# A scan and a mixture of experts on one core: decays, matrix copies, late transfers and the first expert products in another order

## The chip, the cores and the metric

The kernel runs on one core of a Trainium2 chip. The metric is the device time in microseconds of one execution, measured on that core. Three executions of the kernel before were timed; one more was recorded by the hardware profiler.

The core has five instruction streams: PE (TensorE: matrix products, transposes), DVE (VectorE), ACT (ScalarE), POOL (GpSimd) and SP (SyncE, which here only issues transfers). Each runs its own instructions strictly in order, and waits on semaphores for the others. Transfers run on 16 DMA engines. There are two sources of transfers: plain ones, issued by SP, and indirect ones (gathers and scatters of rows by a list of indices), issued by POOL.

## What is computed

`x` is 2 sequences of 4096 tokens with 512 channels, in fp32. A layer norm is followed by two branches: `s`, a long convolution of each channel with a kernel made of 16 decaying exponentials, plus a scaled residual; and `g`, the SiLU of a mixture of experts (8 experts of 512 x 512 with a bias, the two best per token, weighted by a softmax). The output is `x + s * g`.

```python
def _L0_attn_ref(x, delta, alpha, beta, gamma, omega):
    scale = math.sqrt(1.0 / n_state)
    residual = x * omega
    p = jax.nn.sigmoid(delta)
    a = jax.nn.sigmoid(alpha)
    q = 1.0 - p * a
    vander = t[None, None, :] * jnp.log(q)
    kernel = p * beta * jnp.exp(vander)
    k = jnp.einsum('dnl,dn->dl', kernel, gamma * scale)
...
    out = jnp.fft.irfft(x_f * k_f, n=n_fft)[..., :l]
    return jnp.swapaxes(out, -1, -2) + residual

def _L0_ffn_ref(x, We, be, Wg, bg):
    gate_logits = xf @ Wg.T + bg
    topk_vals, topk_idx = jax.lax.top_k(gate_logits, TOP_K)
    gate_w = jax.nn.softmax(topk_vals, axis=-1)
    all_out = jnp.einsum('nd,ehd->neh', xf, We) + be
    sel = jnp.take_along_axis(all_out, topk_idx[:, :, None], axis=1)
    out = jnp.sum(sel * gate_w[:, :, None], axis=1)
...
xn = _layernorm(x, axis=-1)
s = _L0_attn_ref(xn, ...)
g = _silu(_L0_ffn_ref(xn, ...))
x = x + s * g
```

## The kernel before

**Three stages.** The first (about 0 to 100 us) loads `x`, normalises it into the tile `big`, and computes the gate's logits. The second (about 100 to 274 us) is the convolution, while DVE sorts the tokens by expert beside it. The third goes through the experts in 71 tiles of 128 tokens for every token's best expert, and 71 more for the second best.

**The convolution's loop.** The 512 channels are 64 *groups* `g` of 8 channels; four groups make a *set* `u` (16 sets, `i` is the group's place in its set). Every chunk of 64 tokens is multiplied with a 64 x 64 Toeplitz matrix of its channel (`from_chunks`: 16 products, which the profile shows as 32), and what earlier chunks left comes in through 16 states a channel: `states` (products into `ph`) makes a chunk's contribution, DVE multiplies it into `came` and runs two scans over it with the *decays*, and `from_states` adds the scanned states to the outputs `pys` of the *next* set. Once a set, at `i == 1`: `from_states(u)`, `powers_of(u + 2)` on ACT, `states(u + 1)`, the scans for `u + 1`, and `decay_of(u + 2, n)` on ACT, which writes over the decays that scan `n` has just read. At `i == 3`, `turn_powers` transposes the powers on PE and ACT copies them (`w <- pw`). At the set's end `outputs_end` copies the four output banks out of PSUM, three on ACT and one on DVE; a later set's products need those banks.

**The matrices.** `load_toep(g)` loads a group's matrices from DRAM into one half of the partitions (128 KB, issued by SP five groups ahead; six buffers). `double_toep(g)` copies them into the other half, on ACT or on POOL, as `TO_ACT` says by the group's place in its set. It is called two groups ahead, after the products of group `g - 2`.

**Transfers beside the loop.** The dictionary `between`, filled by `at(group, function, ...)`, says what is issued after which group. `store(qi, part)` writes a sixteenth of a quarter of the convolution's output to `s_dram` (256 KB, 64 x 8 rows of 512 bytes). `load_expert(e, half)` loads half of an expert's weights (512 KB) into the parts of `big` that the loop no longer needs. `load_bias(e)` loads a bias, broadcast to all partitions (256 KB), into the first half of the region of `big` from which the third quarter's parts 0 to 7 are stored; the second half, parts 8 to 15, later holds the first tiles' rows and normalised rows. So these loads wait for those stores. All of them stand in SP's one queue with the matrices' loads, in the order in which they are issued. `fetch(i)` is POOL's gather of tile `i`'s rows. Tiles 0 and 1 (`EARLY`) are fetched, normalised and transposed while the loop is still running.

**The experts.** A pass `i` of the loop at the end issues, in this order: `fetch(i + 7)`, statistics of rows (`mean_of`, DVE and ACT), `end_first(i - 2)` (DVE adds the bias to a finished product, POOL scatters the result to `yx_dram`), `normalise` (DVE) of tiles up to a few ahead, `turn` (PE transposes a normalised tile two or three ahead, ACT copies it) and `expert(i)` (PE, four products of 128 x 128 x 512). The normalising runs ahead as far as tile 3 in pass 0, 5 in pass 1, 6 in pass 2 and 8 in pass 3; from pass 4 on the turning runs three tiles ahead instead of two, so that pass 4 turns tiles 6 and 7 ahead of tile 4's product. The expert's number is read at run time, so a product can use any of the eight weights, and a bias addition any of the eight biases: both wait until all of them are there. Products go to five PSUM banks, which are the convolution's banks before.

All engines' instructions are issued through `InOrder`, which keeps the order of the program on each engine; so most lines of the profile bear the number of its one recording line, 59, and are told apart by their tiles.

Of the kernel before, what the change touches and what calls it, by code (L numbers as in the profile page):

```python
# [8 lines left out]
FP = mybir.dt.float32  # L9
# [7 lines left out]
P = 128  # L17
EPS = 1e-5
SX = 4
DOUBLED = 2  # L20
TO_ACT = (0, 2)
IL = 2
AHEAD = 7
READY = 5
# [38 lines left out]
def tile_ssm_then_moe(  # L63
# [179 lines left out]
    def turn(i, pt):  # L243
        xn = xn_b[i % len(xn_b)]
        for k in range(KD):
            io.tensor.transpose(pt[:, k, :], xn[:, k * P : (k + 1) * P], ident)
        io.scalar.copy(xnT_b[i % len(xnT_b)], pt.rearrange("p k t -> p (k t)"))
# [95 lines left out]
    with ExitStack() as ab:  # L343
# [63 lines left out]
        def decay_of(u, n):  # L407

            g = u * NS + 2 * n
            decay = work.tile([P, 2, NP * 2 * C], FP, tag="decay")  # L410
            for i in range(2):
                io.scalar.activation(
                    decay[:, i, :], carry.rearrange("p s c -> p (s c)"), AF.Copy,
                    scale=q_half[:, g + i : g + i + 1],
                )
            return decay


        def turn_powers(u, powers):

            pw = ps_w.tile([P, NS, P], FP, tag="hw", name="pw")
            for i in range(NS):
                io.tensor.transpose(pw[:, i, :], powers[:, i, 0:P], ident)
            w = work.tile([P, NS, P], FP, tag="w", bufs=1)
            io.scalar.copy(w, pw)
            return w
# [60 lines left out]
        def outputs_end(u, sq, pys):  # L487
            to = sq.rearrange("p c (s i r d) -> p s r i d c", i=NS, r=NR, d=NP)
            for r in range(NR):
                copy = io.vector.tensor_copy if r == 1 else io.scalar.copy  # L490
                copy(
                    to[:, u * NS % GQ // NS, r].rearrange("p i d c -> p c i d"),
                    pys[r].rearrange("p i d c -> p c i d"),
                )
# [440 lines left out]
        def load_bias(e):  # L935
            io.sync.dma_start(out=be_sb[:, e, :], in_=b_e[:, e, :].to_broadcast([P, D]))
# [6 lines left out]
        def sq_of(qi):  # L943
            return big[:, (4, 0, 4, 0)[qi], :].rearrange("p (c d) -> p c d", d=QD)
# [13 lines left out]
        def at(n, f, *args):  # L958
            between.setdefault(n, []).append((f, args))
# [19 lines left out]
        for part in range(NC):  # L979
            for qi in range(2):  # L980
                at(GQ * (qi + 1) + part, store, qi, part)
            at(GQ * 3 + part // 2, store, 2, part)
        for e in range(NE):
            for half in range(2):
                n = 2 * e + half
                at(GQ * 2 + 1 + 2 * n if n < NE else GQ * 3 + n, load_expert, e, half)
            at(GQ * 3 + NC // 2 + e // 2, load_bias, e)
        for i in range(EARLY):
            at(G - 6, fetch, i)
            at(G - 4 + i, mean_of, i)  # L990
# [5 lines left out]
        for u in range(NU):  # L996
            pys = banks() if u else pys0

            late = 0 if u else 1
            for i in range(2 * late, NS):  # L1000
                g = u * NS + i
                if g + TB - 1 < G:
                    toeps[g + TB - 1] = load_toep(g + TB - 1)
                if i == 1 + late:
                    from_states(u, pys, powers.pop(u))
                    if u + 2 < NU:
                        powers[u + 2] = powers_of(u + 2)
                    if u + 1 < NU:
                        states(u + 1, w.pop(u + 1))
                        for n in range(2):  # L1010
                            scan(n, decay.pop((u + 1, n)))
                            if u + 2 < NU:
                                decay[u + 2, n] = decay_of(u + 2, n)
                todo = between.pop(g, [])
                for f, args in todo:
                    if f in first_of_group:
                        f(*args)
                if i == 3 and u + 2 < NU:
                    w[u + 2] = turn_powers(u + 2, powers[u + 2])
                from_chunks(u, i, pys, toeps.pop(g))  # L1020
                if g + DOUBLED < G:
                    double_toep(g + DOUBLED)
                for f, args in todo:
                    if f not in first_of_group:
                        f(*args)
            outputs_end(u, sq_of(u * NS // GQ), pys)
        assert not between, between
        for part in range(NC):
            store(3, part)

    with ExitStack() as cc:
        mp = cc.enter_context(tc.tile_pool(name="more", bufs=1))
        ps_t = cc.enter_context(tc.tile_pool(name="ps_t2", bufs=2, space=PSUM))
        ps_e = cc.enter_context(tc.tile_pool(name="ps_e", bufs=5, space=PSUM))
        ps_tab = cc.enter_context(tc.tile_pool(name="ps_tab", bufs=1, space=PSUM))

        def more(n, width, name):
            return [mp.tile([P, width], FP, name=f"{name}{i}") for i in range(n)]

        xn_b += more(2, D, "xn")  # L1040
        xnT_b += more(3, D, "xnT")
        yx_b += more(4, 2 * D, "yx")
        sg_b += more(6, D + SX, "sg")
        x_b += more(FIRST - 5, D, "x")

        n = len(work_list)  # L1050
        for i in range(EARLY, AHEAD):
            fetch(i)
        ready, turned, ended, held = EARLY, EARLY, 0, {}

        def make_ready(upto, before_ends):

            nonlocal ready
            for i in range(ready, min(upto, n - 1) + 1):
                if before_ends:
                    if i < NT:  # L1060
                        mean_of(i)
                else:
                    normalise(i)
                    ready = i + 1

        def made_in_spare(b):

            low, high = (buf.bitcast(BF) for buf in (y_b[b % 2], g_b[b % 2]))
            return [
                low[:, 0 : BC * P].rearrange("p (c t) -> p c t", c=BC),  # L1070
                low[:, BC * P : BC * (P + NT)].rearrange("p (c t) -> p c t", c=BC),
                high[:, 0 : BC * 2 * NT].rearrange("p (c f t) -> p c f t", c=BC, f=2),
            ]

        late = list(range(NT, NT + AHEAD + 1))
        for before_ends in (True, False):
            make_ready(2, before_ends)
        for i in range(n + 1):
            if i + AHEAD < n:
                fetch(i + AHEAD)  # L1080
            to_be = i + 3 + min((i + 1) // 2, READY - 3)
            make_ready(to_be, True)
            ends = range(ended, i - (BEHIND if i < n - 2 else 1) + 1)
            ended = max(ended, ends.stop)
            for e in ends:
                if e < NT:
                    end_first(e, held.pop(e))
                elif e == ends[0]:
                    add_expert(e, held.pop(e))
            if ended >= NT:  # L1090
                for ii in late[: 3 if len(late) > AHEAD else 1]:
                    late.remove(ii)
                    fetch_first(ii)
                if i + AHEAD < n:
                    fetch_first(i + AHEAD)
            make_ready(to_be, False)
            if 0 <= i - TABLES - 2 < NM:
                put(ps_tab)
                if i - TABLES - 2 == NM - 1:
                    table_end(1, y_b[2][:, 0 : 2 * NT].rearrange("p (f j) -> p f j", f=2))  # L1100
            if 0 <= i - TABLES < NM:
                make(1, i - TABLES, made_in_spare)
            for ii in range(turned, min(i + 2 + (i >= 4), n - 1) + 1):
                turn(ii, ps_t.tile([P, KD, P], FP, name="pt"))
                turned = ii + 1
            if i < n:
                held[i] = ps_e.tile([P, D], FP, tag="pe", name="pe")
                expert(i, held[i])
            if ended == NT and ends:
                take_first(NT)  # L1110
                add_bias(NT)
                take_first(NT + 1)
            for e in ends:
                if e >= NT:
                    if e > ends[0]:
                        add_expert(e, held.pop(e))
                    if e + 1 < n:
                        add_bias(e + 1)
                    if e + 2 < n:
                        take_first(e + 2)  # L1120
                    put_out(e)
# [47 lines left out]
```

## Time and profile before

| | us |
|---|---|
| median of 3 executions | 874.09 (872.93 to 882.62) |
| the profiled execution | 874.42 |
| its span, first to last instruction | 872.7 |

```profile
PE 794.3 (91%) x7038; PEld 464.0 (53%) x7038; DVE 598.4 (69%) x1147; ACT 359.6 (41%) x699; POOL 507.4 (58%) x513
PE   3989888888974999999999999998998999999993
POOL 6777310333324357765455456767777777777752
PEclk9899999999997899999999999999999999999997
DMA  4656112889999974456555557668877777888851
```

The first line gives every engine's busy time, share of the span and number of instructions. Below it the span is cut into 40 equal slices of 21.8 us: a digit is the busy share of a slice in tenths, and for PEclk the TensorE clock that was granted. DMA is the mean busy share of the 16 DMA engines. The convolution is in the fifth to the thirteenth slice, the experts' first pass begins in the fourteenth, and the second pass follows it. The DMA engines are at nine tenths or more from the tenth slice to the fourteenth.

The issues, by kind, with the size of one and the median time from issue to landing:

```profile
s_dram<-big SPq DMA_DIRECT2D x64, 256.0 KB, 5.6
toep_b<-k_dram SPq DMA_DIRECT2D x64, 128.0 KB, 4.6
big<-in_w_e SPq DMA_DIRECT2D x16, 512.0 KB, 7.1
big<-in_b_e SPq DMA_DIRECT2D x8, 256.0 KB, 8.6
k_dram<-came_b SPq DMA_DIRECT2D x1, 256.0 KB, 2.3
```

### The profile page before, as it was taken

To read this page: it belongs to the slowest core of one execution; us is meant where nothing else is said; L and a number is where in the kernel's file an instruction comes from. 1 tells how busy PE (TensorE), PEld (TensorE's weight loads), DVE (VectorE), ACT (ScalarE), POOL (GpSimd) and SP (SyncE) were. 2 spreads that over 40 slices of the span, in tenths; PEclk is the share of its full clock that TensorE was granted. 3 is DMA by queue.
4 is the path that set the end of the run, shared out by engine and by line. 5 is a ranking of instruction groups with operands and counts; after the bars stand their busy time and mean duration, and the time that the engine had idled before them with its cause. 6 is when DMAs were issued, how large, how long until landed. Compare 5 with 4: busy or idle time off the path is not lost.

```text
span 872.7 us, 18657 instructions
## 1 busy us (share of the span) xinstructions
PE 794.3 (91%) x7038; PEld 464.0 (53%) x7038; DVE 598.4 (69%) x1147; ACT 359.6 (41%) x699; POOL 507.4 (58%) x513
## 2 busy tenths in 40 slices
PE   3989888888974999999999999998998999999993
PEld 3777777777763455554444445444443444444441
DVE  7878479766683667776566565355787777777786
ACT  6887666575652212222212212133443343433442
POOL 6777310333324357765455456767777777777752
PEclk9899999999997899999999999999999999999997
DMA  4656112889999974456555557668877777888851
GB/s 153 221 210 228 33 45 58 109 211 264 253 237 342 293 235 176 169 176 226 194 203 196 184 203 227 218 219 293 251 250 228 256 255 233 254 253 250 260 198 42
DMA packets 112823, 181.23 MB, mean 208 GB/s; under 512 B 18910, under 2 KB 68446, under 8 KB 112736
## 3 DMA queue, kind: packets, MB, share of 16 engines
q0 software_dynamic: 38128, 127.05, 44.1%
q1 hardware_dynamic: 74608, 52.99, 22.6%
q8 instruction: 58, 0.95, 0.4%
q14 instruction: 29, 0.24, 0.1%
HBM read 112.50 MB, written 73.01 MB: 213 GB/s over the span
## 4 chain that ended last, share of the span: by engine, by line
PE 36%; POOL 17%; issue 15%; DMA 14%; DVE 9%; ACT 8%; SPq 2%; POOLq 0%; DVEq 0%; ACTq 0%
PE pe L59 21%; POOL big L59 6%; PE py L59 5%; POOL out L59 5%; PE pt L59 4%; ACT big L59 4%; DVE came_b L59 4%; DMA yx<-yx_dram,x_idx 3%; DVE big L59 3%; DMA big<-yx_dram,x_idx 3%; POOL sg L59 3%; PE ph L59 2%; DMA toep_b<-k_dram 2%; SPq L59 2%; POOL yx L59 2%
## 5 line engine op out<-in xcount | busy, mean ns | idle before, releaser
L59 PE MATMUL pe<-big,xnT 128*128 x672 | 302.7, 593 | 0.4 <-issue 0.4
L59 PE MATMUL pe<-big 128*128 x464 | 212.0, 600 | 2.2 <-DMA s_dram<-big 2.2
L59 PEld LDWEIGHTS pe<-big,xnT 128*128 128x128 f32 x672 | 121.2, 190 | 122.1 <-issue 122.0
L59 PEld LDWEIGHTS pe<-big 128*128 128x128 f32 x464 | 85.1, 193 | 88.9 <-issue 85.8
L59 ACT ACTIVATE big<-big 128x512 f32<-128x512 f32 x103 | 66.5, 650 | 158.8 <-DVE big L59 154.3
L59 ACT COPY big<-pt 128x512 f32<-128x512 f32 x122 | 68.3, 594 | 90.8 <-PE pt L59 90.8
L59 ACT COPY xnT<-pt 128x512 f32<-128x512 f32 x84 | 48.4, 577 | 130.9 <-PE pt L59 130.4
L59 PE MATMUL py<-big,toep_b 64*64 64x64 f32 x2048 | 83.6, 231 | 20.3 <-ACT toep_b L59 8.3
L59 POOL DMA_INDIRECT out<-big,o_idx x71 | 78.5, 1105 | 39.2 <-DVE big L59 21.2
L59 PEld LDWEIGHTS pt<-ident,big 128*128 128x128 f32 x544 | 73.2, 195 | 49.8 <-issue 24.6
L59 PE MATMUL pt<-ident,big 128*128 128x128 f32 x544 | 86.9, 297 | 8.4 <-DVE big L59 5.8
L59 PEld LDWEIGHTS py<-big,toep_b 64*64 64x64 f32 x2048 | 72.9, 141 | 32.6 <-ACT toep_b L59 10.1
L59 POOL DMA_INDIRECT yx_dram<-big,o_idx x47 | 48.3, 1029 | 57.6 <-DVE big L59 51.2
L59 POOL COPY toep_b<-toep_b 64x512 f32<-64x512 f32 x32 | 23.2, 729 | 79.6 <-DMA toep_b<-k_dram 68.3
L59 POOL TENSOR_SCALAR big<-big,stats 128x512 f32<-128x512 f32 x44 | 55.7, 1343 | 23.5 <-ACT stats L59 9.8
L59 POOL DMA_INDIRECT big<-in_x,x_idx x52 | 51.0, 982 | 26.9 <-issue 13.8
L59 DVE TENSOR_TENSOR big<-pe,big 128x512 f32<-128x512 f32 x47 | 32.5, 691 | 42.4 <-PE pe L59 40.8
L59 PEld LDWEIGHTS pt<-ident,xn 128*128 128x128 f32 x280 | 33.7, 143 | 46.8 <-issue 30.9
L59 POOL DMA_INDIRECT sg<-s_dram,x_idx x42 | 47.2, 1125 | 12.8 <-issue 9.5
L59 PE MATMUL pt<-ident,xn 128*128 128x128 f32 x280 | 43.1, 278 | 11.9 <-DVE xn L59 10.9
L59 DVE TENSOR_TENSOR big<-big 128x512 f32<-128x512 f32 x73 | 50.3, 689 | 3.4 <-ACT big L59 1.9
L59 POOL DMA_INDIRECT big<-yx_dram,x_idx x44 | 43.4, 987 | 14.5 <-issue 13.1
(170 smaller groups left out, 1121.4 us busy)
## 6 DMA issues: line engine op xcount, KB each, us to landing
big<-in_x_rev SPq DMA_DIRECT2D x16, 1024.0 KB, 5.4
s_dram<-big SPq DMA_DIRECT2D x64, 256.0 KB, 5.6
toep_b<-k_dram SPq DMA_DIRECT2D x64, 128.0 KB, 4.6
big<-in_w_e SPq DMA_DIRECT2D x16, 512.0 KB, 7.1
big<-in_b_e SPq DMA_DIRECT2D x8, 256.0 KB, 8.6
out<-big,o_idx POOLq DMA_INDIRECT x71, 4.6
big<-in_x,x_idx POOLq DMA_INDIRECT x52, 3.5
yx_dram<-big,o_idx POOLq DMA_INDIRECT x47, 3.4
```

The costliest lines, as they stand in the source:

```text
L59: return lambda *args, **kwargs: self.order.follow(make(*args, **kwargs))
```

## The change

There are four edits. Their common effect on the engines' totals is nil: every instruction and every transfer stays, on another engine or in another place.

1. *Decays.* `decay_of(u + 2, n)` is issued in the set's fourth group, in front of `turn_powers`, and no longer right behind the scans in the second group.
2. *Copies of matrices.* ACT now copies the matrices of a set's second and third group (`TO_ACT` was the first and third), POOL those of the first and fourth. The copy for the next set's second group, which is called in the fourth group, is issued behind `outputs_end`.
3. *Late transfers.* In groups 48 to 63 the stores of the third quarter are issued one every second group, then one a group, and only parts 12 to 15 and 8 to 11; the experts' weights keep their step of one half every second group to the end of the loop (group 63). Parts 0 to 7 and, behind them, all eight biases are issued after the loop, in front of the fourth quarter's 16 stores.
4. *First expert products.* In passes 0 and 1, `expert(i)` is issued in front of the turning, so that tile 0's product stands before tile 2's turning on PE.

```diff
-TO_ACT = (0, 2)
+TO_ACT = (1, 2)
...
         for part in range(NC):
             for qi in range(2):
                 at(GQ * (qi + 1) + part, store, qi, part)
-            at(GQ * 3 + part // 2, store, 2, part)
+
+        for n, part in zip((0, 2, 4, 6, 7, 8, 9, 10), (12, 13, 14, 15, 8, 9, 10, 11)):
+            at(GQ * 3 + n, store, 2, part)
         for e in range(NE):
             for half in range(2):
                 n = 2 * e + half
-                at(GQ * 2 + 1 + 2 * n if n < NE else GQ * 3 + n, load_expert, e, half)
-            at(GQ * 3 + NC // 2 + e // 2, load_bias, e)
+                at(GQ * 2 + 1 + 2 * n, load_expert, e, half)
...
                             scan(n, decay.pop((u + 1, n)))
-                            if u + 2 < NU:
-                                decay[u + 2, n] = decay_of(u + 2, n)
...
                 if i == 3 and u + 2 < NU:
+                    for n in range(2):
+                        decay[u + 2, n] = decay_of(u + 2, n)
                     w[u + 2] = turn_powers(u + 2, powers[u + 2])
                 from_chunks(u, i, pys, toeps.pop(g))
-                if g + DOUBLED < G:
+                if g + DOUBLED < G and i < 3:
                     double_toep(g + DOUBLED)
...
             outputs_end(u, sq_of(u * NS // GQ), pys)
+            if g + DOUBLED < G:
+                double_toep(g + DOUBLED)
         assert not between, between
+        for part in range(NC // 2):
+            store(2, part)
+        for e in range(NE):
+            load_bias(e)
         for part in range(NC):
             store(3, part)
...
-            for ii in range(turned, min(i + 2 + (i >= 4), n - 1) + 1):
-                turn(ii, ps_t.tile([P, KD, P], FP, name="pt"))
-                turned = ii + 1
-            if i < n:
-                held[i] = ps_e.tile([P, D], FP, tag="pe", name="pe")
-                expert(i, held[i])
+
+            for what in ("turn", "expert") if i >= EARLY else ("expert", "turn"):
+                if what == "turn":
+                    for ii in range(turned, min(i + 2 + (i >= 4), n - 1) + 1):
+                        turn(ii, ps_t.tile([P, KD, P], FP, name="pt"))
+                        turned = ii + 1
+                elif i < n:
+                    held[i] = ps_e.tile([P, D], FP, tag="pe", name="pe")
+                    expert(i, held[i])
```

## Prediction

> **What bounds the kernel now.** I began with the table of forty slices on the page: PE is busy at 0.8 or more nearly everywhere, and its one hole is the two slices from 240 to 284 us (7 and 4 tenths), where the scan's loop hands over to the experts. So I asked for that hole's windows, then for the timelines of PE, SyncE (SP), GpSimd (POOL) and VectorE (DVE) in it.
>
> ```profile
> 240.00:250.00 10.00, 8.46 (x263) 7.02 (x262) 7.14 (x15) 6.31 (x15) 2.25 (x2) 1.00 1.05 244
> 260.00:270.00 10.00, 4.59 (x112) 4.08 (x114) 2.90 (x9) 2.07 (x4) 0.62 (x2) 0.76 1.05 287
> 270.00:280.00 10.00, 4.21 (x78) 3.72 (x75) 3.74 (x8) 2.99 (x7) 6.08 (x7) 0.84 1.05 382
> 280.00:290.00 10.00, 5.94 (x11) 2.95 (x12) 6.06 (x18) 1.76 (x5) 2.13 (x3) 0.54 1.04 329
> 290.00:300.00 10.00, 10.00 (x33) 4.97 (x32) 7.08 (x16) 2.52 (x7) 4.43 (x5) 1.00 1.01 272
> ```
>
> The columns after the stretch are its length, busy time of PE, PEld, DVE, ACT, POOL, the granted clock, the DMA share and GB/s. No engine is full between 260 and 290 us; the DMA engines are, all along.
>
> ```profile
> 262.25 1.12 PE L59 MATMUL py<-big,toep_b 64*64 64x64 f32 x16 [2.68 <-DVE big L59]
> 268.46 3.54 PE L59 MATMUL py<-big,toep_b 64*64 64x64 f32 x64 [3.15 <-POOL toep_b L59]
> 272.79 1.18 PE L59 MATMUL py<-big,toep_b 64*64 64x64 f32 x32 [0.78 <-POOL toep_b L59]
> 281.88 1.09 PE L59 MATMUL pt<-ident,xn 128*128 128x128 f32 x4 [6.90 <-DVE xn L59]
> 285.15 5.66 PE L59 MATMUL pe<-big 128*128 x8 [2.17 <-DMA s_dram<-big]
> 303.14 3.60 PE L59 MATMUL pe<-big,xnT 128*128 x8
> ```
>
> The last two groups' matrices come late (3.15 and 0.78), then the third tile's turning (6.90) and the expert weights (2.17; the name is that of another SP transfer, the weights are what this product needs). From 285.15, where tile 0's product starts, PE is full until about 600 us: what this hand-over gains, the end gains. 303.14 is tile 4's product.
>
> ```profile
> 254.75 2.32 SPq L59 DMA_DIRECT2D big<-in_b_e  x2
> 260.52 0.58 SPq L59 DMA_DIRECT2D toep_b<-k_dram  x1
> 271.22 3.13 SPq L59 DMA_DIRECT2D big<-in_w_e  x4
> 277.16 24.82 SPq L59 DMA_DIRECT2D s_dram<-big  x15
> 267.80 0.61 POOL L59 COPY toep_b<-toep_b 64x512 f32<-64x512 f32 x1 [7.79 <-DMA big<-in_x,x_idx]
> 290.85 0.69 DVE L59 TENSOR_TENSOR big<-pe,big 128x512 f32<-128x512 f32 x1 [3.33 <-PE pe L59]
> 296.17 0.78 DVE L59 TENSOR_SCALAR xn<-yx,sm 128x512 f32<-128x512 f32 x1
> ```
>
> The last matrices' load is issued at 260.52, behind biases; the last weights at 271 to 274; POOL's copy for group 61 sits behind tile 1's row gather. At 290.85 DVE adds the bias to tile 0's product; at 296.17 it normalises tile 7.
>
> **Decays and copies in the loop.** In the waits of PE between 100 and 195 us the first line below is the largest (us in total, times, longest); the others are ACT's timeline around the longest.
>
> ```profile
> PE py L59 <- ACT toep_b L59: 7.1, 7, 2.4
> 112.87 0.91 ACT L59 ACTIVATE decay<-mask,q_half 128x256 f32<-128x256 bf16 x2 [0.58 <-DVE came_b L59]
> 113.80 0.62 ACT L59 COPY toep_b<-toep_b 64x512 f32<-64x512 f32 x1
> 114.44 0.58 ACT L59 COPY w<-pw 128x512 f32<-128x512 f32 x1
> 114.93 1.59 ACT L59 COPY big<-py 128x512 f32<-128x512 f32 x3
> ```
>
> ScalarE (ACT) cannot copy the next set's first matrix before its decays, which wait for DVE's scan. The change gives that copy to POOL, so this wait goes; but the decays, moved only as far as the fourth group, still stand in front of the turned powers (w) and the output copies, and PE needs the first output copy for the last quarter of the next set's first group. What is late next is therefore the output copy, 0.62 us earlier than now: a wait of 2.4 becomes one of about 1.8. Of the seven, four are long (2.38, 2.05, 0.83, 1.16) and three short (0.18 to 0.26); one more of 1.18 stands at 251. Two of the long ones lie between 131 and 153 us, where DVE is busy 20.58 of 22 us and would hold PE instead; three times 0.62 and the short ones' 0.67 are 2.5. Copies per engine stay equal (two each a set). The second matrix's copy now stands on ACT behind the outputs; PE needs it only after 1.2 + 1.6 us of other products, so I cost it at nothing (0.62 a set, were that cover gone). Against the gain, POOL's copy now falls beside the scans more often: the pair of scans at 110.13 took 2.71 beside a POOL copy of 1.27, where other pairs took 2.34. Four times 0.37 is 1.5. Net 1.0 gained, bounds -2 (no gain, six such scans) to +5 (0.62 in all eight).
>
> The Trainium skill speaks against this part: "SBUF — State Buffer", section "SBUF: two separate sides", says that GpSimd and a VectorE operation with two SBUF inputs lock each other out of one port pair for a whole instruction. The 2.71 and 1.27 agree.
>
> **The late transfers.** The bytes stay; their order changes. From group 48 SP today issues two stores a group, then biases and weights: with 1.07 us for a 262 KB store and 0.54 for a matrix load (at 244 GB/s, the window of 240 to 250, which holds nothing else), it has 2.7 us of work a group against PE's 2.57 (sets begin at 231.20 and 241.46), and from group 56 about 4. After the change, two groups hold two matrices, a store and a weight half (524 KB at 319 GB/s, below): 3.8 us against 5, and groups 55 to 58 9.7 against 10. So matrices come in time, and tile 0's and 1's gathers land sooner, and the 3.15 and 0.78 go, with 1.35 of slow clock (3.54 where 64 products otherwise take 2.19). The 2.68 at 262.25 is DVE's own chain and stays. PE's last group then ends 1.0 + 3.15 + 0.78 + 1.35 = 6.3 earlier than 273.97, at 267.7.
>
> The price: all eight biases now come last, behind eight stores they overwrite. The first bias addition waits for all of them. Queued behind it on DVE are the normalising of tiles 6 and up; on POOL, tile 0's scatter and behind it the gather for tile 10. SP's last 16 stores go behind the biases too; their first reader is a gather at 535 us, so nothing. When do the biases land? The rate first: between 254.75 and 285.15 went 8 biases, 8 weight halves, 2 matrices, 10 row gathers of 262 KB and about 2 stores, 9.7 MB in 30.4 us, 319 GB/s. The last matrices' load goes when group 57's products end, at 256.8 now and 255.8 with the loop's 1.0. From there: 9 stores 9.7 us, the load 0.5, 3 weight halves 4.9, 8 biases 6.6, 9 gathers 7.4: 29.1 us, and 1.2 to land (the page's lone 256 KB transfer takes 2.3, of which 1.07 moves). Biases at 286.1. Bounds: 22 us if all 8.5 MB went at the 382 of one window, 279; 39 us if SP's 6.2 MB go as the last stores do (15 in 24.82 us, 158 GB/s), 296.
>
> **The first products.** Tile 0's product no longer stands behind tile 2's turning, and it needs the output copies, which end 3.2 after PE's turnings begin (273.9 to 277.1): 270.9. Weights, with 10.6 of those 29.1 us ahead of them (five gathers among it), land at 267.6. So 6.90 and 2.17 go entirely. From tile 0 to tile 4 PE takes 18.0 now, 15.8 without the slow first product (5.66 against 3.44): tile 4 could start at 286.7. But tile 4's product stands behind the turnings of tiles 6 and 7, and tile 7 is normalised 6.1 after the first bias addition starts (290.85 to 296.95), or 5.5 where the root before tile 6 is already done (0.56). Biases at 286.1, plus 5.5, plus 0.7 for the turning: tile 4 at 292.3, instead of 303.14. That is 10.8 earlier, less 1.35 for a clock that falls in the new stall of some 5 us: **9.5 gained**. The profiled execution took 874.42 us (span 872.7), 0.3 over the median of 874.09: 864.9, say 865.
>
> **Rivals.** *No barrier.* The biases land by 280.5; then tile 4 starts at 286.7, 16.4 earlier: 858. For: 382 GB/s for ten microseconds. Against: that window holds almost no 512-byte stores, and nine are ahead of the biases. 0.15.
>
> *The loop pays.* Every one of 14 scans runs beside a POOL copy: 14 x 0.37 = 5.2 lost and nothing gained, in place of 1.0 gained; 6.2 off the gain gives 871. For: 110.13. Against: at 197 and 207 us POOL's copies lie clear of the scans. The lock that the Trainium skill's "SBUF — State Buffer" describes would do exactly this. 0.13.
>
> *Slower: the biases starve.* POOL's gathers run on their own queue and take engine time ahead of SP's 9 stores, 3 weight halves and 8 biases. Stores from 294 to 304 us were issued at five in ten microseconds, 131 GB/s; 6.2 MB so take 47 us, the biases land at 304, tile 4 starts at 310.2, with the clock 8.4 later than now: 883. It decides once they land after 295.6; at 158 GB/s it is about a draw. For: both queues are full in the hole. Against: around 300 each tile also scatters 512 KB, which before the first bias addition none can. The Trainium skill's "DMA: Bandwidth & Descriptors", section "Queues, rings and completion order", has each engine take turns between the queues, packet by packet, which alone would leave SP its turn. 0.14.
>
> **How the numbers follow.** The forecast has 0.58, its own range 861 to 869 (loop -2 to +5, biases 282 to 290). A measurement here tells 1%, 8.7 us, from no change: the line is 865.4. Of the forecast 0.31 lies below it; with the first rival faster is 0.46. Within 1%: 0.27 of the forecast, 0.13, and half the last rival, 0.47. Slower 0.07. Range 857 to 873: it leaves out half of the first rival and most of the last.
>
> **What would show it.** No wait of PE for matrices after 262; tile 0's product before 273; the first bias addition waiting for a DMA until 284 to 288 and PE idle before the turnings of tiles 6 and 7; waits for output copies where waits for matrices were at 114 to 157. Wrong it is if the bias addition never waits, if PE stalls in the loop on POOL's copies, or if a shift at 303 us does not reach the end.

## The result, and the profile after

| | before | changed |
|---|---|---|
| median, same chip (22 executions each) | 876.25 | 868.12 (858.94 to 881.31) |
| the profiled execution | 874.42 | 863.34 |
| its span | 872.7 | 861.6 |

The ratio is 0.987, 95% interval 0.9848 to 0.9892. In two later sessions, on two different chips, the changed kernel was run again: 0.9946 (0.9899 to 0.9993) and 0.9943 (0.9908 to 0.9977); there the kernel before took 911.56 and 882.09 us. All ratios and intervals here leave out executions over 1.5% above the fastest of their kernel (six of the changed kernel's 22, none of the 22 before); with every execution counted, the medians of the three sessions give 0.991, 0.990 and 0.994. So the change is faster in all three sessions, by 1.3%, 0.5% and 0.6%.

The page after, the slices of PE and of the DMA engines:

```profile
PE   3999987889877999999999999998999999999993
DMA  4657222999989975555565557678888888888851
```

The hole is less deep: the two slices of 7 and 4 tenths from 240 to 284 us are now a 7 and a 7 (twelfth and thirteenth). Four of the same stretches as windows, in the columns used before:

```profile
260.00:270.00 10.00, 6.37 (x177) 5.93 (x173) 5.03 (x13) 3.57 (x6) 5.00 (x6) 0.83 1.10 315
270.00:280.00 10.00, 7.80 (x24) 4.04 (x24) 4.97 (x14) 3.93 (x10) 3.22 (x4) 0.83 1.08 353
280.00:290.00 10.00, 10.00 (x34) 5.05 (x33) 4.76 (x13) 1.60 (x5) 1.64 (x2) 1.00 1.06 303
290.00:300.00 10.00, 8.61 (x30) 4.24 (x29) 6.25 (x16) 2.80 (x7) 4.67 (x6) 1.00 1.07 319
```

From 280 to 290 PE is full, where it did 5.94 of 10 us before; the DMA engines are as full as they were. PE's own timeline over the end of the loop and the first tiles (start, busy, what, and in brackets the idle time ahead with what ended it):

```profile
253.07 1.55 PE L59 MATMUL ph<-big,w 64*32 64x128 f32 x61 [1.48 <-issue]
254.55 2.25 PE L59 MATMUL py<-big,toep_b 64*64 64x64 f32 x67
258.45 2.02 PE L59 MATMUL py<-big,toep_b 64*64 64x64 f32 x61 [1.65 <-issue]
260.40 1.21 PE L59 MATMUL py<-came_b,powers 32*64 32x128 f32 x64
261.54 0.33 PE L59 MATMUL py<-big,toep_b 64*64 64x64 f32 x3
265.50 4.52 PE L59 MATMUL py<-big,toep_b 64*64 64x64 f32 x93 [3.63 <-issue]
269.95 1.09 PE L59 MATMUL pt<-ident,big 128*128 128x128 f32 x8
273.24 5.26 PE L59 MATMUL pe<-big 128*128 x8 [2.20 <-ACT big L59]
...
290.39 0.60 PE L59 MATMUL pt<-ident,xn 128*128 128x128 f32 x4
291.65 0.63 PE L59 MATMUL pt<-ident,xn 128*128 128x128 f32 x4 [0.66 <-DVE sm L59]
293.01 3.69 PE L59 MATMUL pe<-big,xnT 128*128 x8 [0.73 <-issue]
```

The waits for GpSimd's copies (3.15 and 0.78), for the third tile's rows (6.90) and for the weights (2.17) are gone, and so is the 2.68 for DVE. In the first one's place stands a wait of 3.63 that the profile names "issue": PE waits there for nothing that the profile shows another engine or a transfer to signal. Two more of this name, 1.48 and 1.65, stand ahead of it. Tile 4's product (293.01) starts 10.13 us earlier than before. SP's and DVE's timelines of the same time:

```profile
257.60 2.19 SPq L59 DMA_DIRECT2D big<-in_w_e  x3
259.84 12.81 SPq L59 DMA_DIRECT2D s_dram<-big  x8
272.74 2.27 SPq L59 DMA_DIRECT2D big<-in_b_e  x1
```

```profile
287.09 0.69 DVE L59 TENSOR_TENSOR big<-pe,big 128x512 f32<-128x512 f32 x1 [4.82 <-DMA s_dram<-big]
290.95 0.56 DVE L59 TENSOR_SCALAR xn<-yx,sm 128x512 f32<-128x512 f32 x1
```

The last weights go out at 257.60, then eight stores that take SP 12.81 us, then the biases, and the first bias addition waits 4.82 for a transfer. (Its name is that of a store on the same queue; what this addition needs are the biases behind it.) At 290.95 tile 7 is normalised, and its turning at 291.65 is what PE waits for.

In the loop, PE's waits between 100 and 195 us, and ACT around the place that was shown before:

```profile
PE py L59 <- ACT big L59: 5.4, 4, 2.2
PE py L59 <- DVE big L59: 2.3, 1, 2.3
PE py L59 <- POOL toep_b L59: 1.1, 2, 0.9
```

```profile
111.83 0.91 ACT L59 ACTIVATE decay<-mask,q_half 128x256 f32<-128x256 bf16 x2 [0.58 <-DVE came_b L59]
112.64 0.56 ACT L59 COPY w<-pw 128x512 f32<-128x512 f32 x1
113.11 1.61 ACT L59 COPY big<-py 128x512 f32<-128x512 f32 x3
114.74 1.26 ACT L59 COPY toep_b<-toep_b 64x512 f32<-64x512 f32 x2
```

No matrix copy stands between decays and turned powers any more, and PE waits for output copies (`big`, on ACT and DVE) where it waited for ACT's matrices. The three lines of waits sum to 8.8. All of PE's waits in the stretch sum to 11.5 us before and 13.6 after, so sums of waits do not show a gain; what the exchange brings is seen in the sets' lengths (e9, e10).

What was gained at tile 4 stays: the addition of tile 20's bias moves from 374.4 to 364.0, tile 60's from 527.9 to 517.8, the end of the span from 872.7 to 861.6.

### The profile page after: what moved, and what is told of

It reads as the page before. It is cut to its first block, busy times and chain, and to the rows that moved or that the text cites. A ratio compares the mean times of both kernels' runs of the same rounds, so it can differ in the third digit from the quotient of the medians.

```text
span 861.6 us, 18686 instructions
## 1 busy us (share of the span) xinstructions
PE 786.1 (91%) x7038; PEld 458.9 (53%) x7038; DVE 601.6 (70%) x1147; ACT 358.1 (42%) x699; POOL 509.1 (59%) x513
## 2 busy tenths in 40 slices
DMA packets 112823, 181.23 MB, mean 210 GB/s; under 512 B 18910, under 2 KB 68446, under 8 KB 112736
## 4 chain that ended last, share of the span: by engine, by line
PE 35%; POOL 16%; issue 14%; DMA 14%; DVE 11%; ACT 7%; SPq 2%; POOLq 0%; DVEq 0%; ACTq 0%
PE pe L59 20%; PE py L59 6%; POOL big L59 6%; ACT big L59 5%; DMA big<-yx_dram,x_idx 4%; DVE big L59 4%; PE pt L59 4%; POOL out L59 4%; DMA yx<-yx_dram,x_idx 3%; DVE came_b L59 3%; POOL sg L59 3%; PE ph L59 3%; SPq L59 2%; DMA out<-big,o_idx 2%; DMA s_dram<-big 2%
## 5 line engine op out<-in xcount | busy, mean ns | idle before, releaser
L59 POOL DMA_INDIRECT out<-big,o_idx x71 | 75.8, 1067 | 38.7 <-DVE big L59 20.5
L59 PE MATMUL py<-big,toep_b 64*64 64x64 f32 x2048 | 79.2, 230 | 18.8 <-issue 8.1
L59 PEld LDWEIGHTS py<-big,toep_b 64*64 64x64 f32 x2048 | 70.7, 142 | 28.9 <-issue 13.4
```

The costliest lines, as they stand in the source:

```text
L59: return lambda *args, **kwargs: self.order.follow(make(*args, **kwargs))
```

## The experiments

Every ratio is to the kernel before on the same chip: e1 to e4 on one (before 879.94), e5 to e8 on a second (911.56), e9 to e12 on a third (882.09). The edits are numbered as in the section on the change. "Carried states" below are the products `py<-came_b` with which a set begins; set 15's mark the last set, at 263.3 before and at 260.4 in the changed kernel's first trace.

**e1, edit 3 alone.** The stores, weights and biases as changed; loop and first products as before.

```diff
-            at(GQ * 3 + part // 2, store, 2, part)
+        for n, part in zip((0, 2, 4, 6, 7, 8, 9, 10), (12, 13, 14, 15, 8, 9, 10, 11)):
+            at(GQ * 3 + n, store, 2, part)
...
-                at(GQ * 2 + 1 + 2 * n if n < NE else GQ * 3 + n, load_expert, e, half)
-            at(GQ * 3 + NC // 2 + e // 2, load_bias, e)
+                at(GQ * 2 + 1 + 2 * n, load_expert, e, half)
...
+        for part in range(NC // 2):
+            store(2, part)
+        for e in range(NE):
+            load_bias(e)
```

> The kernel before with the change's late transfers alone. Theory A (the hand-over is paced by the DMA engines, and in the changed kernel by the biases, which must all land before the first bias addition): nearly the whole gain is here. Tile 0's product waits for tile 2's turning and starts near 275.5 us; the first bias addition waits for a DMA until about 288; tile 4's product starts at 294 to 295; 8 to 9 us faster than before (ratio 0.990). Rival B (the first products in front of the turning are what frees PE): tile 0's product still starts after 280 and no more than 4 us are gained (0.995 or above). Rival C (the loop's decays and copies make the gain): 5 us or less.

Measured: 875.03 us, 0.9942 (0.9912 to 0.9972). That lies between theory A's ratio of 0.990 and rival B's 0.995: a part of the gain, and by the medians the largest that any single edit brings. By the medians it is 4.9 us, just within the 5 of rival C; what speaks against that rival is e2. Tile 0's product starts after 280, as rival B has it (283.77), but only since this execution's whole loop ran later: it is 12.8 us after set 15's carried states, where it is 21.8 before.

**e2, edits 1 and 2 alone**, with transfers and first products as before.

```diff
-TO_ACT = (0, 2)
+TO_ACT = (1, 2)
...
-                            if u + 2 < NU:
-                                decay[u + 2, n] = decay_of(u + 2, n)
...
+                    for n in range(2):
+                        decay[u + 2, n] = decay_of(u + 2, n)
...
-                if g + DOUBLED < G:
+                if g + DOUBLED < G and i < 3:
...
+            if g + DOUBLED < G:
+                double_toep(g + DOUBLED)
```

> The kernel before with the decays and the copies of matrices moved, nothing else. Theory A: waits for matrices on ACT become waits for output copies, the loop gains 1 to 2 us, and the hand-over, which is paced by bytes, shifts with it: 1 us faster (ratio 0.998 to 1.000). Rival C: all eight waits for the copy go, 5 us or more (0.994 or below). Rival D (the port that POOL and DVE share): slower by 2 to 4 us (1.002 to 1.005).

Measured: 876.74 us, 0.9976 (0.9945 to 1.0007). A gain of 0.6% or more is outside the interval; whether there is any is left to e6, e9 and e10.

**e3, edit 4 alone.**

```diff
+            for what in ("turn", "expert") if i >= EARLY else ("expert", "turn"):
...
```

> The kernel before with the first two expert products in front of the turning, nothing else. Theory A: tile 0's product waits for the last weight half, which lands at about 285 as before; the turning then comes behind it: no change (ratio 0.999 to 1.001). Rival B: 2 to 7 us faster (0.992 to 0.998).

Measured: 881.41 us, 1.0003 (0.9976 to 1.0031). PE's timeline shows why: with the transfers of before, the product put in front waits itself, for its weights (named, again, by another transfer of the queue):

```profile
291.82 5.61 PE L59 MATMUL pe<-big 128*128 x8 [8.79 <-DMA s_dram<-big]
```

With the new transfers it changes what PE waits for. In e1, where the turning still goes first, PE waits for tile 2's rows, and tile 0's product comes right behind:

```profile
282.65 1.02 PE L59 MATMUL pt<-ident,xn 128*128 128x128 f32 x4 [4.14 <-DVE xn L59]
283.77 4.85 PE L59 MATMUL pe<-big 128*128 x8
```

Set 15's carried states begin at 271.0 in this trace, so the product starts 12.8 after them; in the changed kernel, at 273.24, it starts 12.8 after them too, held by other waits.

**e4, the barrier taken away.** The changed kernel, with tiles 6 and 7 normalised in pass 2, in front of the first bias addition on DVE.

```diff
+            if i == EARLY:
+                to_be = 7
             make_ready(to_be, True)
+            if i == EARLY:
+                make_ready(to_be, False)
```

> The changed kernel, with tiles 6 and 7 normalised in front of the first bias addition (passes 2 and 3 of the experts' loop), so that DVE's wait for the biases no longer stands ahead of their turning. Theory A: the bias addition still waits until about 287, but tile 4's product starts at 287 instead of 293, and the end moves by the same 6 us: about 17 us faster than before (ratio 0.980 to 0.982). Rival E (the biases' landing costs nothing, as PE is held by rows or by something later anyway): tile 4 stays near 293, the ratio at 0.987.

Measured: 868.78 us, 0.9893 (0.9847 to 0.9938). PE no longer waits in front of tiles 6's and 7's turnings (`x8` without a wait):

```profile
296.77 1.04 PE L59 MATMUL pt<-ident,xn 128*128 128x128 f32 x8
297.65 3.60 PE L59 MATMUL pe<-big,xnT 128*128 x8
```

But tile 4's product, 297.65, starts 31.5 after set 15's carried states, against 32.6 in the changed kernel: by these two traces the barrier was worth 1.1 us, not the 5.6 that the prediction priced it at. The interval excludes the 0.980 to 0.982 that the large price would have given (rival E of the expectation, not theory A).

**e5, the changed kernel again; e6, without edits 1 and 2; e7, without edit 4.** All on the second chip.

> The changed kernel once more, on the chip of the next three, as their measure: ratio to before 0.985 to 0.991, whatever the theory. Its trace: PE waits of the kind that the profile calls issue again at the same instructions (after 67 records in the last set but one, after 3 records of the last set's second group), 5 us together.

> The change without its first two edits: late transfers and first products only. Theory A: slower than the changed kernel by what the loop gained, 1 to 2 us (ratio to before 0.988 to 0.991). Rival C (the loop makes a third of the gain or more): 4 us slower than the changed kernel (0.992 or above).

> The change without its fourth edit: tile 2's turning stands ahead of tile 0's product. Theory A: tile 0's product starts 1 to 3 us later than in the changed kernel, but the turning of tile 7, behind the biases, still sets tile 4's product: 0 to 1.5 us slower than the changed kernel. Rival B: the whole delay reaches the end, 3 us or more.

Measured: e5 902.21 us, 0.9946; e6 907.0 us, 0.9982 (0.9944 to 1.0020); e7 901.24 us, 0.9927 (0.9888 to 0.9966). By these ratios leaving the loop edits out costs 0.36%, 3.3 us, between theory A's 1 to 2 and rival C's 4; e6's ratio is the one that rival C asked for (0.992 or above). The intervals of e5 and e6 overlap, so this does not decide between them. Leaving the first products out costs nothing that the intervals can tell. In e6 the old waits are back: PE waits 7.2 us for ACT's matrix copies between 100 and 195. In e7 tile 0's product starts 18.1 after set 15's carried states, behind a wait of 3.41 for tile 2's rows, and 15.9 in e5: 2.2 later, as theory A has it.

e5 itself missed both its marks. Its ratio lies above the 0.985 to 0.991 that was expected, and of the two waits named issue, of 5 us together, it shows 0.21 and 1.44 at the two places, and 3.5 more in seven pieces behind the second.

**e8, SP held.** Kernel e4 with the first of the last 16 stores, which needs the last set's outputs, put in front of the eight late stores and the biases, so that SP issues nothing while PE ends the loop.

```diff
+        store(3, 0)
         for part in range(NC // 2):
             store(2, part)
...
-        for part in range(NC):
+        for part in range(1, NC):
             store(3, part)
```

> The kernel with rows ahead, and SP held in front of the eight stores and the biases: the first of the last 16 stores, which waits for the loop's last outputs, is issued ahead of them. Theory F (PE's waits of the kind issue at the end of the loop are its instruction fetch, which stands behind SP's stores in the DMA engines): from the last set's from_states to tile 0's product 9 to 10 us instead of 13, the two issue waits of 5 us shrink to under 2; the biases then land near 30 us after the last set's start instead of 26.7 and hold tile 5 instead of tile 4; 1 to 4 us faster than the changed kernel (ratio to before 0.983 to 0.986). Rival G (these waits have nothing to do with other transfers): they stay at 5 us, tile 0's product stays at 13, and the later biases make it 2 to 5 us slower than the changed kernel.

Measured: 907.99 us, 0.9984 (0.9948 to 1.0019). That is 3.5 us slower than e5, as rival G has it, and theory F's gain is excluded. From its trace (span 921.9) the order of events is read, and lengths only as rough sizes. PE's wait named issue is still there, 3.81 at the same product, though SP issued nothing between 279.75 and 294.48:

```profile
279.30 0.33 PE L59 MATMUL py<-big,toep_b 64*64 64x64 f32 x3
283.45 4.43 PE L59 MATMUL py<-big,toep_b 64*64 64x64 f32 x87 [3.81 <-issue]
...
318.57 1.12 PE L59 MATMUL pt<-ident,xn 128*128 128x128 f32 x4 [6.16 <-ACT big L59]
```

So the late stores do not make that wait (tile 0's product starts 16.3 after the carried states, later than either theory has it). The hold put the biases' landing at 316.2, and the last line is then the barrier as the prediction meant it: the turning behind the first bias addition holds PE by 6.16.

**e9, edit 1 alone; e10, edit 2 alone; e11, the changed kernel once more.**

```diff
e9
-                            if u + 2 < NU:
-                                decay[u + 2, n] = decay_of(u + 2, n)
...
+                    for n in range(2):
+                        decay[u + 2, n] = decay_of(u + 2, n)
...
e10
-TO_ACT = (0, 2)
+TO_ACT = (1, 2)
...
-                if g + DOUBLED < G:
+                if g + DOUBLED < G and i < 3:
...
+            if g + DOUBLED < G:
+                double_toep(g + DOUBLED)
```

> Edit 1 alone: the decays in the set's fourth group; copies, transfers and first products as before. Read on the sets that run at a granted clock of 1.00 throughout: before, the first set takes 9.47 to 9.51 us and the sixth 9.12; with both loop edits 8.95 and 8.37. Theory A (what counts is only that the first group's copy does not stand behind the decays on ScalarE; either edit alone frees it, and the second adds nothing): the first and sixth sets at or below 9.0 and 8.5, PE's waits for ScalarE's matrix copies in the first six sets below 1.5 us in total, where they are 6.6 before, ratio 0.996 to 0.9985. Theory B (the copies count, and decays in front of the turned powers delay the output copies): first set 9.3 or more, ratio 0.999 to 1.002. Theory N (the loop's gain was the granted clock of single executions): ratio 1.000, within 0.2%, and sets as before.

> Edit 2 alone: GpSimd copies a set's first group, ScalarE the second, behind the output copies; the decays stay behind the scans. Theory A: first and sixth sets at or below 9.0 and 8.5, PE's waits for ScalarE's matrix copies below 1.5 us, ratio 0.996 to 0.9985. Theory B: the same, and decays alone nothing. Theory P (GpSimd's copies beside the scans cost what the prediction charged, 0.37 a pair): VectorE's busy time in the first six sets rises from 49.6 to 51 or more, and the ratio is 1.000 or above. Theory N: ratio 1.000, within 0.2%.

> The changed kernel once more, to stand beside the two single edits on one chip. By the runs so far 0.986 to 0.995; if theory A holds for both single edits, it lies 0.4% to 1% below each of them, which is the late transfers' part.

Measured: e9 879.23 us, 0.9973 (0.9948 to 0.9998); e10 879.78 us, 0.9977 (0.9947 to 1.0007); e11 876.5 us, 0.9943. The intervals are wide for effects of this size; the traces are sharper. As windows, the first and second set (from one set's carried states to the next set's), where every clock is 1.00: first of e6, which has the loop of before, then of e9, then of e10.

```profile
109.30:118.81 9.51, 6.93 (x230) 5.99 (x229) 7.25 (x10) 7.59 (x16) 2.30 (x2) 1.00 0.19 45
118.81:127.93 9.12, 8.48 (x265) 7.19 (x261) 5.75 (x9) 6.39 (x16) 0.92 (x1) 1.00 0.28 61
```

```profile
105.96:114.92 8.96, 6.60 (x229) 5.79 (x228) 6.70 (x10) 7.71 (x16) 1.47 (x2) 1.00 0.24 48
114.92:123.55 8.63, 8.10 (x266) 6.94 (x262) 6.30 (x9) 6.42 (x15) 1.49 (x2) 1.00 0.27 62
```

```profile
105.58:114.54 8.96, 6.62 (x230) 5.81 (x229) 6.69 (x10) 7.10 (x15) 2.15 (x2) 1.00 0.21 48
114.54:123.15 8.61, 8.08 (x264) 6.93 (x261) 6.30 (x9) 6.33 (x15) 1.15 (x2) 1.00 0.27 63
```

The sixth set, also at 1.00, takes 9.12, 8.39 and 8.36. Each edit alone so shortens each of the three sets by 0.5 to 0.8 us (9.51 to 8.96, 9.12 to 8.61, 9.12 to 8.36), and e2, with both, has the same lengths: 8.95, 8.61, 8.36. So what counts is that ACT's copy of the first group does not stand behind the decays, and one of the two edits is enough (theory A); no wait for ACT's matrix copies is left in the first six sets of either. The theory on GpSimd for e10 (P) fell: VectorE's busy time in the first six sets is 49.1, where the kernel before has 49.6, and of the loop's 16 pairs of scans one takes 2.71 instead of 2.34, where before two do. So GpSimd's moved copies did not slow the scans. The part of e11's expectation that set it 0.4% to 1% below the single edits was a little high: it lies 0.30% and 0.34% below them.

**e12, the DMA engines quieter.** The changed kernel with the last three weight halves behind the first of the last 16 stores as well, so that little is moved while PE ends the loop.

```diff
-                at(GQ * 2 + 1 + 2 * n, load_expert, e, half)
+                if n < 13:
+                    at(GQ * 2 + 1 + 2 * n, load_expert, e, half)
...
+        store(3, 0)
+        for n in range(13, 16):
+            load_expert(n // 2, n % 2)
         for part in range(NC // 2):
             store(2, part)
...
-        for part in range(NC):
+        for part in range(1, NC):
             store(3, part)
```

> The changed kernel with its last three weight halves moved from the end of the loop to behind the loop, after the first store of the fourth quarter, which waits for the last set's outputs; SP so issues nothing between the last matrices and the loop's end. Theory S (PE's waits named issue in the last two sets, 6.9 to 9.8 us in all so far, come from the load on the DMA engines at that time): the DMA share between set 14 and the end of the loop falls clearly below 1.0, PE's issue waits from there to the end of the loop sum to 2 us or less, and its last group ends 7.5 us or less after the start of set 15, where the changed kernel took 9.6 and 12.2. Theory F (they belong to the place in the instruction stream, whatever the load): 4 us or more remain at the same instruction, the third behind the 64 products of the last set's carried states. Either way tile 0's product then waits for its weights, and the time says nothing of the waits: ratio 0.99 to 1.005.

Measured: 882.26 us, 0.9995 (0.9968 to 1.0021). Two windows and PE's timeline:

```profile
265.00:270.00 5.00, 3.43 (x128) 3.05 (x127) 3.53 (x12) 4.45 (x7) 0.49 (x1) 1.00 0.68 182
270.00:275.00 5.00, 4.27 (x93) 4.28 (x93) 2.44 (x7) 0.29 (x1) 3.82 (x5) 0.66 0.42 113
```

```profile
265.05 2.04 PE L59 MATMUL py<-big,toep_b 64*64 64x64 f32 x61 [1.65 <-issue]
268.15 0.33 PE L59 MATMUL py<-big,toep_b 64*64 64x64 f32 x3
270.73 4.48 PE L59 MATMUL py<-big,toep_b 64*64 64x64 f32 x93 [2.24 <-issue]
286.89 5.78 PE L59 MATMUL pe<-big 128*128 x8 [10.67 <-DMA big<-in_w_e]
```

The DMA share falls to 0.68 and 0.42, and still PE waits 2.24 at the same product, and 1.65 and 0.94 at the two places ahead of it: 4.8 us in all where theory S asked for 2 or less. So theory S fell as it was put, and so did theory F, which asked for 4 us or more at that product alone. In the changed kernel's three traces the wait there is 3.63, 1.44 (e5) and 4.18 (e11), with the DMA engines full each time; whether the load has a part in its length is not settled by the 2.24 here.

## Why the prediction was right, step by step

The forecast was 865 us, 9.5 less than before; the same chip gave 868.12 against 876.25, 8.1 less. The term it rested on, the landing of the biases, came as put. The terms of PE's own way to tile 4 were off by more than 4 us in all. Tile 4's product waits for the later of the two, the biases with the rows behind them or PE itself, and PE was still the earlier one, by 0.66 us. That margin is luck: had PE been a little later, it and not the biases would have set the time, as it did in e7, where the turnings of tiles 6 and 7 wait for nothing.

- *The biases' landing.* Forecast 286.1, seen as the first bias addition at 287.09. The sum of bytes over a measured rate held: the windows of 260 to 290 show 303 to 353 GB/s, and the forecast used 319. Tile 4's product followed 5.9 us behind, where 5.5 and 0.7 were worked out: 293.01 instead of 292.3. In e5 and e11 the addition comes 27.9 and 28.5 after set 15's carried states, where it is 26.7 in the first trace, so this term is within 2 us there too.
- *The barrier's price.* Here the step failed. The forecast had PE ready for tile 4 at 286.7 and held until 292.3, by 5.6. In the trace PE ran without a gap from tile 0's product to 290.99, the end of tile 6's turning. Without the barrier e4 gained 1.1; in the changed kernel's own trace the two turnings in a row, as in e4, would have put tile 4's product at 291.3, 1.7 earlier. PE was itself that late for two reasons that follow.
- *PE's last group* was to end at 267.7, and ended at 269.95 (tile turnings begin there). From set 14's carried states to there PE took 19.9 us, where it took 20.9 before and the forecast asks for 15.6; that set 14 began 2.0 earlier than forecast made up for half of the difference. The late transfers did remove 3.15 and 0.78, and the 2.68 that was to stay went too. But the two sets got waits named issue of 1.48, 1.65 and 3.63, 6.8 in all, which the forecast did not have, and the slow clock that was to go stayed: the last 93 products take 4.52, and at the forecast's 2.19 for 64 it would be 3.2. The waits are not new with the transfers: e2, whose transfers are those of before, waits 3.90 at the same product as the 3.63. In the kernel before, the longest of this name between 240 and 275 was 1.24. If what PE waits for is its instructions (last section), the last set's wait was hidden there: their packet had come by 265.56, and PE stood until 268.46 for GpSimd's copy in any case. A removed wait uncovered the next one.
- *Tile 0's product* was counted at 3.44 without its slow clock, and the slow clock stayed: 5.26, in windows at 0.83. So the 2.2 that the forecast took off between tiles 0 and 4 did not come. In return the 1.35 set aside for a clock that falls in the new stall wasn't spent: at 280 to 300 the clock is 1.00, and there is hardly a stall.
- *The first products.* Right that 6.90 and 2.17 go. The transfers bring the weights in time and the rows earlier; without edit 4, PE still waits 4.14 (e1) and 3.41 (e7) for tile 2's rows, and edit 4 takes that wait away. But no gain of time from edit 4 is measured: e3 alone gives nothing, and e5 and e7 differ by nothing that can be told. After the last group the output copies hold tile 0's product by 2.20, as forecast (3.2 from the start of the turnings, seen 3.29).
- *The loop.* Forecast 1.0 with bounds of -2 to +5; the timings give 0.24% (e2, 2.1 us of 880) and 0.36% (e5 beside e6, 3.3 of 907). The step's own reading was good: 0.62 a set, and nothing where DVE is full (third to fifth set together: 32.16 us in e6, 32.26 in e2, though there at a clock of 0.95 and 0.89 for two of them). What was mis-sized is the price set against it, 1.5 for GpSimd's copies beside scans. Of the 16 pairs of scans, three (at 109.08, 181.23 and 190.18) took 2.71, each beside a copy; before, two did (110.13 and 235.61), and in both traces the others took 2.34 or 2.35. That is one pair more, 0.37 and not 1.5. Without the price the step says 2.5, which fits the 2.1 and 3.3. The rule of the Trainium skill's "SBUF — State Buffer", section "SBUF: two separate sides", agrees with the pairs that met a copy, and has nothing to act on in the changed kernel's others.
- *The rivals.* "No barrier" needed biases by 280.5, and they came 6.6 later. "The loop pays" needed 14 slow scans. "The biases starve" needed them after 295.6; SP's 16 late issues got their turn beside GpSimd's gathers. Held back, as in e8, they hold PE by 6.16, a wait of the size that the barrier was priced at.

Of the signs named at the end of the forecast, the matrices, the bias addition and the output copies came as put; tile 0's product started 0.24 late of 273; PE was idle for 0.66 ahead of tile 7's turning, and not at all ahead of tile 6's, instead of some 5 in all.

**What the parts add up to.** From set 15's carried states to the addition of tile 20's bias the five traces with the transfers of before (before, e2, e3, e9, e10) take 109.8 to 112.7 us, mean 111.3; seven with the new ones (after, e1, e4 to e7, e11) take 102.3 to 107.2, mean 105.1. So edit 3 is worth 6.2 us there; by the timings the loop edits bring 2 to 3, and edit 4 nothing that shows. By the ratios alone edit 3 brings less: 5.1 us in e1, and in e6, together with edit 4, 1.6, which is not clear of nothing.

**What stays open.** Why the ratios give 1.3% in the first session and 0.5% and 0.6% in two others; the medians of all executions lie closer together (0.9%, 1.0% and 0.6%). The six sets from the seventh to the twelfth, where the DMA engines are full, took 63.3 us in the trace of before, 65.0 in the changed kernel's first and 67.3 to 73.9 in the others but e8 (77.3), so one pair of traces can carry several microseconds of chance. And what sets the length of the waits named issue isn't known. No kernel measured was faster than the changed one by more than the intervals.

## What to carry to other kernels

A transfer that sets a time can be placed well by the bytes issued ahead of it over a rate measured in the same stretch: this came within 1 us of 287. Before a wait is priced, ask whether the engine that would wait is itself ready then: take the waits away one by one on its own timeline, and put a slow clock and a wait for its own instructions back in, since here these left 1.1 to 1.7 us of a barrier of 5.6. Small gains are better read from the lengths of equal stretches at an equal clock than from sums of waits, and one chip's percentage is not another's.

## What the runs showed of the hardware

The waits named issue look like PE waiting for its own instructions. The trace's third class of transfers, beside SP's and GpSimd's, are instruction packets; the larger of their two queues:

```profile
q8 instruction: 58, 0.95, 0.5%
```

That is 58 packets of 16 KB, about one for every 121 of the 7038 recorded products. In the changed kernel the seven waits named issue of over 0.6 us that end between 231 and 266 us stand 127 or 128 recorded products apart, and each time PE goes on 1.25 to 1.73 us after such a packet has come. For the last of them, PE stops at 261.87, behind the third of the last set's products with its matrices; an instruction packet starts at 263.14 and takes 1.11, and PE goes on at 265.50. In e12 PE stops at 268.48, the packet runs from 268.09 to 269.29, and PE goes on at 270.73. A wait of this name, of 1.4 to 4.2 us, stands at the same product in all eleven traces in which PE does not wait there for GpSimd's copy (all but before, e3 and e9), whether the DMA engines are full or not. That these packets are what PE waits for is an inference from their times; no run took them away. The Trainium skill's "Runtime: NRT & Kernel Launch", section "Instruction fetch mechanics", has every engine fetch its instructions in blocks of 16 KiB on a queue of its own, ahead of use, and calls the cost mostly hidden. The packets' size agrees; if these waits are the fetch, that it is mostly hidden does not hold at the end of this loop.

Chips can differ by more than the change brings: the kernel before took 876.25, 879.94, 911.56 and 882.09 us in the four sessions. On the chip of the 911.56 the extra time lies behind the addition of tile 60's bias: from there to the end of the span e5 takes 376.2 us, the changed kernel's first trace 343.8 and e11 341.3.
